# Local attention: the output projection in split halves for two batches at a time, values after the normed q and k, a second buffer for transposed q and k

## The chip, the cores and the metric

The kernel runs on one core of one Trainium2 chip, in one launch. The metric is the device time of that launch in microseconds (us). Engines are named PE (TensorE, matrix products; PEld is its loading of weights), DVE (VectorE), ACT (ScalarE), POOL (GpSimd) and SP (SyncE, which issues most DMAs).

## The reference, cut to what matters

The program is six blocks in a row on `x` of 64 batches x 128 tokens x 128 features, each with a layer norm in front and its input added behind. The third, the one that changes, is two layers of local attention with a gated feed-forward part:

```python
h = shift_token(x)                        # half of the features from the token before
q, k, v = jnp.split(h @ wqkv, 3, axis=-1) # 8 heads of 64
q = l2norm(q) * qs; k = l2norm(k) * ksc
q, k = rotary_xpos(q, k)
o = local_attention(q, k, v)              # a token sees itself and the 64 before it
x = x + o @ wo                            # 512 -> 128: the product that changes
h = layernorm(shift_token(x)) * lg + lb
a, g = jnp.split(h @ w1 + b1, 2, axis=-1)
x = x + (a * gelu(g)) @ w2 + b2
```

## The kernel before, in words

Each block is a class (B1 to B6), and each has a stage of the span to itself, but for its set-up, which runs within the stage ahead. All of `x` stays in SBUF. Stage 3 (class B3, line 1123) works on 16 chunks of 4 batches (`CB = 4`). For each chunk and each of the two layers there are four units, one a batch (`unit`, line 1182), and behind the fourth one the feed-forward part of the chunk (`ffn`, line 1246). That makes 32 chunk-layers and 128 units. `emit` (line 1296) starts one unit a step, layer 1 of a chunk two chunks behind its layer 0 (`LAG = 2`), and each `yield` in the text below moves what follows to a later step, so that some dozen units are under way at a time.

**Products.** A product in float32 is one call of `mm` and two records in the trace. Where speed matters, the kernel splits each float32 operand into a high and a low half of the type F32R, and `mm3` makes three products, high x high, high x low and low x high, that add up in PSUM. `wsplit` makes the halves of a weight: a copy and a subtraction on DVE. In stage 2 (B2) the output product is already made so, for two batches at a time: the tiles `ush`, `usl` and the weight `cBsh`, `cBsl`.

**A unit** (128 tokens, 8 heads) goes so: from the split input `yh`, `yl` come q and k (two PSUM tiles named B) and, right behind them, v (a PSUM tile named a), which ACT copies to `va` (8 buffers). ACT squares q and k (`fsq`); DVE sums the squares (`n2`) and makes the two rotary products `t1` and `t2`; POOL adds them, and scales them by the norm. D1 = 3 steps later PE transposes the result (`B<-k_eye,t`), and ACT copies it to `qkT`, which has one buffer. Then come the scores (`B<-qkT`) with the mask (`band`), the softmax (`mx`, `prob`, `dn` on DVE, ACT and POOL), its transposes (`probT` on ACT) and the product with `va`. ACT copies that to the tile `f_oT`, one for the four batches of a chunk.

**ffn**, behind the fourth unit, begins with the output projection: 4 float32 products of 512 columns over the whole chunk, which two DVE instructions of 64 x 512 add to the residual `ys`. Then it transposes, normalises, makes the two split products with `w1`, the gelu and the product with `w2`.

**Order.** Nothing of this runs in the order of the text. The calls are recorded (class `Recorder`) and, at the end of each stage, a planner (`order`) lays them out: each engine takes, of the instructions whose inputs and buffers are ready in its estimate, the one with the smallest position in the text plus an offset from a table (`PRIO`, by stage, engine and tile). PE's products are grouped up to 940 ns of estimate, and changes of the array's form and of ACT's function table carry penalties (`STICK`, `STICKX`, `STICKSET`). Each engine then works through its list strictly in order, so a late input holds what is listed behind it. SP issues DMAs in order too. All instructions are issued from one line of `flush` (L607), so the profile tells them apart by tiles.

PSUM has 8 banks: 5 for the tiles B and 3 for the tiles a. The input halves `yh`, `yl` have two buffers each, `t1` two, `t2` and `f_oT` one.

**Set-up of stage 3** runs in stage 2: `f_wo` is loaded as it is; `k_rot`, `k_band` and the two layers of `f_wqkv` pass one after the other through the single buffer `stage`; the two layers of `f_w1` through two buffers `stage1`.

Of the kernel before, what the change touches and what calls it, by code (L numbers as in the profile page):

```python
# [18 lines left out]
P = 128  # L19
NBATCH = 64  # L20
T = 128
# [28 lines left out]
H6, O6 = (2, 26)  # L50
LAG = 2
D1, D2, D3, D4 = (3, 1, 3, 1)
SIDES = ("left", "right")


def layout(inputs):
# [118 lines left out]
    for j, (s, g) in enumerate(((sc, 8.0), (1.0 / sc, 1.0))):  # L175
# [31 lines left out]
        "DVE:stage1<f_lg,stage1": -4000, "DVE:w1sh<stage1": -5400,  # L207
    },
    3: {
        "STICK": 1934, "STICKSET": 11024, "STICKX": -10655, "POOL:yl<yh,ys": 20400, "PE:B<wqsh,yh": 200,  # L210
        "PE:a<wqsh,yh": 1100, "ACT:va<a": 5600, "ACT:fsq<B": 37000, "DVE:n2<fsq": 500, "DVE:t1<B,rot": 9500,
        "DVE:t2<B,rot": 12900, "ACT:n2<n2": 68000, "DVE:ln6<xt": -19500, "DVE:lnmv<ln6": -5700,
        "ACT:lnr<eps5,lnmv": -32200, "ACT:lnr<lnr": -27600, "PE:a<htok,k_eye": -41300, "ACT:ys<a": 27300,
        "DVE:ys<a": -7000, "PE:B<k_eye,t1": 400, "ACT:qkT<B": -71200, "PE:B<qkT": 1100, "PE:B<band,eyeb": -45400,
        "DVE:mx<B": 3200, "DVE:dn<prob": 48100, "POOL:prob<dn,prob": 35200, "PE:B<k_eye,prob": -28500,
        "ACT:probT<B": 23000, "PE:a<probT,va": 8500, "ACT:f_oT<a": -68100, "DVE:ln6<a": -8400,
        "PE:a<ftok,k_eye": -33200, "ACT:fTh<a": -106100, "DVE:fTl<a,fTh": 8500, "PE:a<fTh,w1sh": 3000,
        "ACT:gl<a,f_b1": 15800, "ACT:gl<gl": 18200, "DVE:gl<a,f_b1,gl": -15300, "PE:a<f_w2,gl": 5700,
        "DVE:htok<a,f_b2,ys": 84900, "DVE:xt<a,xt": -1500, "PE:a<probT": 32400, "DVE:win0l<probT,win0h": 75300,
    },  # L220
    4: {
        "STICK": 22428, "STICKSET": 12816, "STICKX": -72497, "ACT:xTh<a": -25500, "DVE:xTl<a,xTh": 5000,
# [419 lines left out]
def build(tc, a, out, nb=NBATCH, blocks="123456"):  # L642
# [11 lines left out]
    def t(shape, tag, dt=F32, bufs=None):  # L654
        if isinstance(cur["wk"], Ahead):
            return nc.alloc(cur["wk"].pool, shape, dt, "ahead_" + tag, nm(tag), 1, 1)
        return nc.alloc(cur["wk"], shape, dt, tag, nm(tag), bufs, 2)
# [25 lines left out]
    def load(name, eng=None):  # L683
        ap = a[name]
        x = wt(ap.shape, name)
        (eng or nc.sync).dma_start(x, ap)
        return x
# [12 lines left out]
    def wsplit(parts, shape, name):  # L700

        hi, lo = wt(shape, name + "h", F32R), wt(shape, name + "l", F32R)
        for x, ix in parts:
            V.tensor_copy(hi[ix], x)
            V.tensor_tensor(lo[ix], x, hi[ix], ALU.subtract)
        return hi, lo
# [15 lines left out]
    def stage(ap):  # L722
        x = t(ap.shape, "stage", bufs=1)
        nc.sync.dma_start(x, ap)
        return x
# [397 lines left out]
    class B3(Block):  # L1123
# [2 lines left out]
        ahead = AH[1]  # L1126

        def load(s):
            s.wo, s.w2 = load("f_wo"), load("f_w2")
            s.lg, s.lb, s.b1, s.b2 = (load(n) for n in ("f_lg", "f_lb", "f_b1", "f_b2"))  # L1130

        def setup(s):
            s.rot = wt([P, 2, 2, 2, 64], "rot")
            krot, qsr = stage(a["k_rot"]), t([P, 2, 2, 64], "stage2", bufs=1)
            nc.sync.dma_start(qsr, a["f_qs"].to_broadcast([P, 2, 2, 64]))
            for l in range(2):
                for j in range(2):
                    V.tensor_tensor(s.rot[:, l, 0, j], krot[:, 0, j].rearrange("p a d -> p (a d)"),
                                    qsr[:, l, j], ALU.mult)
                    for u in range(2):  # L1140
                        V.tensor_tensor(s.rot[:, l, 1, j, 32 * u:32 * u + 32], krot[:, 1, j, u],
                                        qsr[:, l, j, 32 - 32 * u:64 - 32 * u], ALU.mult)
            s.band = cast(stage(a["k_band"]), "band", BF16)
            parts = []
            for l in range(2):
                w1 = t([P, 6, P], "stage1")
                nc.sync.dma_start(w1, a["f_w1"][:, l])
                p1 = ps("a")
                for g in range(6):
                    mm(p1[:, g:g + 1], w1[:, g], s.lb[:, l:l + 1])  # L1150
                V.tensor_tensor(s.b1[:, l], p1[:, 0:6], s.b1[:, l], ALU.add)
                V.tensor_scalar(w1, w1, s.lg[:, l:l + 1], None, ALU.mult)
                parts.append((w1, (slice(None), l)))
            s.w1 = wsplit(parts, [P, 2, 6, P], "w1s")
            s.wqkv = wsplit(((stage(a["f_wqkv"][:, l]), (slice(None), l)) for l in range(2)), [P, 2, 1536], "wqs")

        def halves(s, y):
# [24 lines left out]
        def unit(s, c, l, b):  # L1182
            d = s.d[c]
            hs = [x[:, b] for x in d["hs"]]
            qk, v = [ps("B"), ps("B")], ps("a")
            for j in range(2):
                mm3(qk[j], hs, [w[:, l, j * 512:(j + 1) * 512] for w in s.wqkv])
            mm3(v, hs, [w[:, l, 1024:1536] for w in s.wqkv])
            va = t([P, 8, 64], "va", bufs=8)
            nc.scalar.copy(va.rearrange("p h d -> p (h d)"), v)  # L1190
            sq = t([P, 2, 512], "fsq", bufs=1)
            for j in range(2):
                act(sq[:, j], qk[j], AF.Square)
            n2 = t([P, 16], "n2")
            V.tensor_reduce(n2, sq.rearrange("p j (h d) -> p (j h) d", h=8), AX.X, ALU.add)
            t1, t2 = t([P, 2, 8, 64], "t1"), t([P, 2, 8, 64], "t2", bufs=1)
            for j in range(2):
                V.tensor_tensor(t1[:, j], qk[j].rearrange("p (h d) -> p h d", h=8),
                                s.rot[:, l, 0, j].unsqueeze(1).to_broadcast([P, 8, 64]), ALU.mult)
                r4 = s.rot[:, l, 1, j].unsqueeze(1).to_broadcast([P, 8, 64]).rearrange("p h (u d) -> p h u d", u=2)  # L1200
                V.tensor_tensor(t2[:, j].rearrange("p h (u d) -> p h u d", u=2),
                                qk[j].rearrange("p (h u d) -> p h u d", h=8, u=2)[:, :, ::-1], r4, ALU.mult)
            G.tensor_tensor(t1, t1, t2, ALU.add)
            act(n2, n2, AF.Ln, bias=tiny)
            act(n2, n2, AF.Exp, scale=-0.5)
            G.tensor_scalar(n2, n2, 1e12, None, ALU.min)
            tv = t1.rearrange("p j h d -> p (j h) d")
            G.tensor_tensor(tv, tv, n2.unsqueeze(2).to_broadcast([P, 16, 64]), ALU.mult)
            for _ in range(D1):
                yield  # L1210
            qkT = t([P, 2, 4, T], "qkT", bufs=1)
            for j in range(2):
                tp = ps("B")
                for g in range(4):
                    tr(tp[:, g * T:(g + 1) * T], t1[:, j, 2 * g:2 * g + 2].rearrange("p h d -> p (h d)"), eye)
                nc.scalar.copy(qkT[:, j].rearrange("p g t -> p (g t)"), tp)
            for _ in range(D2):
                yield
            sc = [ps("B"), ps("B")]
            nc.join(True)  # L1220
            for g in range(4):
                for i in range(2):
                    r = slice(64 * i, 64 * i + 64)
                    mm(sc[i][:, g * T:(g + 1) * T], qkT[r, 0, g], qkT[r, 1, g], start=g == 0, stop=False)
            nc.join(False)
            for i in range(2):
                mm(sc[i], eyeb, s.band.unsqueeze(1).to_broadcast([P, 4, P]), start=False)
            p, dn = softmax8(sc, 1.0, T, (0, 1))
            normalise(p, dn, T)
            for _ in range(D3):  # L1230
                yield
            pt = transp8(p, T, "B")
            for _ in range(D4):
                yield
            u = ps("a")
            for g in range(4):
                for i in range(2):
                    mm(u[64 * i:64 * i + 64, g * T:(g + 1) * T], va[:, 2 * g + i], pt[:, 4 * i + g])
            if b == 0:
                d["oT"] = t([P, 4, W], "f_oT", bufs=1)  # L1240
            nc.scalar.copy(d["oT"][:, :, b * T:(b + 1) * T], u.rearrange("p (g t) -> p g t", g=4))
            if b == CB - 1:
                yield
                yield from s.ffn(c, l)

        def ffn(s, c, l):
            d = s.d[c]
            ys, yv = d["ys"], s.halves(d["ys"])
            w = ps("a")
            for g in range(4):  # L1250
                mm(w, s.wo[:, l, g], d["oT"][:, g], start=g == 0, stop=g == 3)
            w3 = w.rearrange("p (b t) -> p b t", b=CB)
            for i in range(2):
                V.tensor_tensor(yv[i], w3[64 * i:64 * i + 64], yv[i], ALU.add)
            yield
            p = ps("a")
            for b in range(CB):
                tr(p[:, b * T:(b + 1) * T], ys[:, b, 0:T], eye)
# [624 lines left out]
```

## Time and profile before

| what | value |
|---|---|
| median of 3 runs | 3488.49 us (3481.11 to 3489.39) |
| the profiled execution's own time | 3487.8 us |
| its span in the profile | 3486.0 us |
| granted PE clock, mean | 0.978 |
| stage 3: first to last product | about 1041 to 2351 us of the span |
| table loads on ACT between 1040 and 2340 us | 62, 79.5 us |

The page's first part gives each engine's busy time over the whole span. Those shares mix six stages with different limits; the tables by stretch give them for stage 3 alone. A row of the timeline has the start, the length, the engine, the line, the operation, the tiles written and read, the shape, and how many equal instructions were merged. A group by shape has busy time in all, the mean length in ns, and the engine's idle time just ahead of its instructions with what ended it. A row of the waits names the engine and tile that waited, what ended the wait, and the total, the number and the longest of such waits.

### The profile page before, as it was taken

The numbers are of one execution on the slowest core, as the hardware profiler recorded it, in microseconds if no ns is written. First come the engines' busy times: TensorE is split into PE (matmuls) and PEld (weight loads), VectorE is DVE, ScalarE is ACT, GpSimd is POOL, SyncE is SP. The second block draws the span as 40 slices with busy tenths as digits, with TensorE's granted clock in tenths as the row PEclk, the third lists the DMA queues.
The fourth block names the chain that finished last, engine by engine and source line by source line (L and its number), as shares of the span: only waits on it lengthen the run. The fifth ranks groups of instructions, "written<-read, shape, count | busy, mean of one in ns | idle before, by whom it ended". The sixth has DMA issues, their size and how long they took to land. (4 is left out here: it accounts for less than half of the span.)

```text
span 3486.0 us, 72432 instructions
## 1 busy us (share of the span) xinstructions
PE 3309.0 (95%) x26754; PEld 2504.7 (72%) x26754; DVE 3022.0 (87%) x6794; ACT 2587.3 (74%) x6272; POOL 1873.6 (54%) x1953
## 2 busy tenths in 40 slices
PE   5999999999998899999999999987999998999999
PEld 4877777777876677677777777755777776677776
DVE  7999788888878789888988888867999998999886
ACT  5888556666657788888888888855767775877785
POOL 2212023332328476676776766637899996544541
PEclk9999899999999999999999999997999998999999
DMA  5344210000000000000000000000000001000000
GB/s 133 88 91 98 68 46 20 10 15 10 14 6 1 1 1 1 1 1 1 1 1 1 1 1 1 1 20 7 1 1 1 1 1 31 10 16 19 16 11 16
DMA packets 43522, 67.13 MB, mean 19 GB/s; under 512 B 9520, under 2 KB 29330, under 8 KB 43171
## 3 DMA queue, kind: packets, MB, share of 16 engines
q1 hardware_dynamic: 42595, 61.98, 7.4%
q8 instruction: 213, 3.49, 0.4%
q14 instruction: 138, 1.13, 0.1%
q10 hardware_dynamic: 576, 0.53, 0.1%
HBM read 24.72 MB, written 4.19 MB: 8 GB/s over the span
## 5 line engine op out<-in xcount | busy, mean ns | idle before, releaser
L607 POOL TENSOR_TENSOR prob<-prob,dn 128x616 f32<-128x616 f32 (+1 forms) x256 | 398.9, 1558 | 471.6 <-DVE dn L607 181.1
L607 POOL TENSOR_TENSOR t<-t,t 128x1024 f32<-128x1024 f32 x128 | 304.7, 2381 | 265.4 <-DVE t L607 223.1
L607 DVE TENSOR_REDUCE dn<-prob 128x8 f32<-128x616 f32 (+1 forms) x384 | 356.6, 929 | 79.8 <-ACT prob L607 77.2
L607 DVE TENSOR_TENSOR t<-B,rot 128x512 f32<-128x512 f32 x512 | 331.6, 681 | 44.1 <-POOL t L607 19.5
L607 DVE TENSOR_REDUCE mx<-B 128x4 f32<-128x308 f32 (+1 forms) x512 | 281.7, 574 | 47.7 <-PE B L607 43.0
L607 ACT COPY probT<-B 77x512 f32<-77x512 f32 (+1 forms) x512 | 288.2, 617 | 36.1 <-PE B L607 31.3
L607 ACT ACTIVATE prob<-B,mx 128x128 f32<-128x128 f32 x1024 | 288.1, 392 | 24.7 <-DVE mx L607 24.2
L607 PEld LDWEIGHTS B<-k_eye,prob 128*77 128x77 f32 (+1 forms) x2048 | 234.6, 144 | 86.8 <-issue 44.9
L607 PE MATMUL B<-k_eye,prob 128*77 128x128 f32 (+1 forms) x2048 | 284.8, 276 | 4.6 <-ACT qkT L607 1.3
L607 POOL TENSOR_TENSOR probN<-prob,dn 128x512 f32<-128x512 f32 (+1 forms) x256 | 176.6, 714 | 141.6 <-PE s L607 104.8
L607 POOL TENSOR_TENSOR t<-t,n 128x1024 f32<-128x1024 f32 x128 | 243.6, 1903 | 4.8
L607 ACT ACTIVATE prob<-s,mx 128x77 f32<-128x77 f32 x768 | 190.8, 366 | 60.9 <-DVE mx L607 49.1
L607 ACT ACTIVATE prob<-prob 128x308 f32<-128x308 f32 x320 | 151.5, 483 | 88.7 <-DVE prob L607 87.5
L607 ACT ACTIVATE feat<-fp,fb 128x512 f32<-128x512 f32 x256 | 163.2, 708 | 33.8 <-PE fp L607 31.5
L607 ACT COPY qkT<-B 128x512 f32<-128x512 f32 x256 | 149.6, 590 | 48.9 <-PE B L607 47.2
L607 POOL TENSOR_TENSOR L<-gs,L 128x512 f32<-128x512 f32 x128 | 163.8, 1281 | 17.4 <-ACT gs L607 9.1
L607 PEld LDWEIGHTS B<-k_eye,t 128*128 128x128 f32 x1024 | 125.7, 142 | 63.7 <-issue 27.6
L607 DVE TENSOR_REDUCE n<-fsq 128x16 f32<-128x1024 f32 x128 | 154.8, 1209 | 16.2 <-ACT fsq L607 12.3
L607 DVE TENSOR_TENSOR am<-fp,k_tri 128x512 f32<-128x512 f32 x256 | 159.0, 675 | 6.7 <-PE fp L607 6.7
L607 POOL TENSOR_TENSOR qnl<-qn,qnh 128x512 fp32r<-128x512 f32 x32 | 44.9, 1407 | 221.8 <-ACT qnh L607 221.8
L607 PE MATMUL B<-ctxbd,qp 128*128 128x154 f32 x1024 | 164.0, 296 | 0.0
L607 DVE TENSOR_TENSOR_SCAN L<-x,k_eye 128x512 f32<-128x512 f32 x128 | 155.2, 1213 | 9.4 <-PE x L607 5.9
(389 smaller groups left out, 10691.0 us busy)
## 6 DMA issues: line engine op xcount, KB each, us to landing
qx<-qnh SPq DMA_DIRECT2D x128, 128.0 KB
qx<-qnl SPq DMA_DIRECT2D x128, 128.0 KB
ctxbd<-ctxbd SPq DMA_DIRECT2D x16, 308.0 KB
xt<-x SPq DMA_DIRECT2D x16, 256.0 KB
out<-xt SPq DMA_DIRECT2D x16, 256.0 KB
ctxT<-ctxT SPq DMA_DIRECT2D x16, 235.6 KB
stage<-f_wqkv SPq DMA_DIRECT2D x2, 768.0 KB
ctxk<-ctx SPq DMA_DIRECT2D x16, 77.0 KB
```

The costliest lines, as they stand in the source:

```text
L607: f(*a, **k)
```

## The change

- The output projection is made with split halves, for two batches at a time: ACT writes the high half `f_oTh`, DVE the low half `f_oTl`, and behind every second unit PE makes 4 x 3 products of 256 columns, which two DVE instructions of 64 x 256 add to the residual. It leaves `ffn` and stands at the end of `unit`.
- The weight `f_wo` is no longer loaded as it is, but through the buffer `stage` and split into `fwosh`, `fwosl`. `stage1` has one buffer in place of two.
- The product for v and its copy stand behind the norm and rotation of q and k, three steps later; `va` has 5 buffers in place of 8.
- `qkT` has two buffers in place of one.
- The table of offsets for stage 3 is another, so that the whole stage is laid out anew.

```diff
+VA, QKB, T2B = (5, 2, 1)
...
-            s.wo, s.w2 = load("f_wo"), load("f_w2")
+            s.w2 = load("f_w2")
...
-                w1 = t([P, 6, P], "stage1")
+                w1 = t([P, 6, P], "stage1", bufs=1)
...
+            s.wo = wsplit([(stage(a["f_wo"]), slice(None))], [P, 2, 4, P], "fwos")
...
-            qk, v = [ps("B"), ps("B")], ps("a")
+            qk = [ps("B"), ps("B")]
             for j in range(2):
                 mm3(qk[j], hs, [w[:, l, j * 512:(j + 1) * 512] for w in s.wqkv])
-            mm3(v, hs, [w[:, l, 1024:1536] for w in s.wqkv])
-            va = t([P, 8, 64], "va", bufs=8)
-            nc.scalar.copy(va.rearrange("p h d -> p (h d)"), v)
...
             for _ in range(D1):
                 yield
-            qkT = t([P, 2, 4, T], "qkT", bufs=1)
+            v = ps("a")
+            mm3(v, hs, [w[:, l, 1024:1536] for w in s.wqkv])
+            va = t([P, 8, 64], "va", bufs=VA)
+            nc.scalar.copy(va.rearrange("p h d -> p (h d)"), v)
+            qkT = t([P, 2, 4, T], "qkT", bufs=QKB)
...
-            if b == 0:
-                d["oT"] = t([P, 4, W], "f_oT", bufs=1)
-            nc.scalar.copy(d["oT"][:, :, b * T:(b + 1) * T], u.rearrange("p (g t) -> p g t", g=4))
+            if b % 2 == 0:
+                d["oT"] = [t([P, 4, 2 * T], n, F32R, 1) for n in ("f_oTh", "f_oTl")]
+            hi, lo = (x[:, :, b % 2 * T:b % 2 * T + T] for x in d["oT"])
+            u = u.rearrange("p (g t) -> p g t", g=4)
+            nc.scalar.copy(hi, u)
+            V.tensor_tensor(lo, u, hi, ALU.subtract)
+            if b % 2 == 0:
+                return
+            o = d["oT"]
+            yield
+            w, b2, yv = ps("a")[:, :2 * T], slice(b - 1, b + 1), s.halves(d["ys"])
+            for g in range(4):
+                mm3(w, [x[:, l, g] for x in s.wo], [x[:, g] for x in o], start=g == 0, stop=g == 3)
+            for i in range(2):
+                V.tensor_tensor(yv[i][:, b2], w[64 * i:64 * i + 64].rearrange("p (b t) -> p b t", b=2), yv[i][:, b2],
+                                ALU.add)
             if b == CB - 1:
                 yield
                 yield from s.ffn(c, l)
...
-            w = ps("a")
-            for g in range(4):
-                mm(w, s.wo[:, l, g], d["oT"][:, g], start=g == 0, stop=g == 3)
-            w3 = w.rearrange("p (b t) -> p b t", b=CB)
-            for i in range(2):
-                V.tensor_tensor(yv[i], w3[64 * i:64 * i + 64], yv[i], ALU.add)
-            yield
```

The table `PRIO[3]`, lines 209 to 220, is replaced as a whole; `STICK` goes from 1934 to 10959, `STICKSET` from 11024 to 49265, `STICKX` from -10655 to -74220.

More of the change, by code (lines that the diff above doesn't have):

```diff
@@ L209 @@
     3: {
[L210 to L219, printed above, removed]
+        "STICK": 10959, "STICKSET": 49265, "STICKX": -74220, "ACT:yh<ys": 8000, "PE:B<wqsh,yh": 16300,
+        "ACT:fsq<B": 218100, "DVE:n2<fsq": 27600, "DVE:t1<B,rot": 26700, "DVE:t2<B,rot": 23500,
+        "ACT:n2<n2,tiny": 3100, "DVE:ln6<xt": 49600, "ACT:lnr<eps5,lnmv": -112900, "ACT:lnr<lnr": 3700,
+        "DVE:htok<lnmv,lnr,xt": -12900, "PE:a<htok,k_eye": 7300, "ACT:ys<a": 26600, "DVE:ys<a": 4100,
+        "PE:a<wqsh,yh": 11500, "ACT:va<a": -23200, "PE:B<k_eye,t1": -400, "ACT:qkT<B": -198300, "PE:B<qkT": -4000,
+        "PE:B<band,eyeb": -900, "DVE:mx<B": -11400, "DVE:dn<prob": 81500, "DVE:dn<dn": 23600,
+        "PE:B<k_eye,prob": -50000, "ACT:probT<B": 10800, "PE:a<probT,va": -7300, "ACT:f_oTh<a": -128400,
+        "DVE:f_oTl<a,f_oTh": 8400, "PE:a<f_oTh,fwosh": -134500, "PE:a<f_oTl,fwosh": 1800, "DVE:ys<a,ys": -111900,
+        "PE:a<k_eye,ys": -17500, "DVE:ln6<a": -9100, "DVE:ftok<a,lnmv,lnr": -6600, "PE:a<ftok,k_eye": -7100,
+        "ACT:fTh<a": 6600, "DVE:fTl<a,fTh": 8700, "PE:a<fTh,w1sh": 7900, "ACT:gl<a,f_b1": -43500,
+        "DVE:gl<a,f_b1,gl": -6700, "PE:a<f_w2,gl": 4800, "DVE:bselb<k_bsel": -3700, "DVE:mF<a,m_gw": 61800,
+        "DVE:win0h<probT": 13100, "DVE:win1l<probT,win1h": 94700,
     },
@@ L1195, in unit @@
             V.tensor_reduce(n2, sq.rearrange("p j (h d) -> p (j h) d", h=8), AX.X, ALU.add)
-            t1, t2 = t([P, 2, 8, 64], "t1"), t([P, 2, 8, 64], "t2", bufs=1)
+            t1, t2 = t([P, 2, 8, 64], "t1"), t([P, 2, 8, 64], "t2", bufs=T2B)
             for j in range(2):
```

## The prediction

> **What bounds the kernel now.** I read the engines' busy line, then busy time by stretch of the span, then the starts of products in the timeline, then groups by shape, then the waits. First the busy line, and three stretches of stage 3 (local attention), the one that changes; its first product starts near 1041 us, its last ends near 2351 us:
>
> ```profile
> PE 3309.0 (95%) x26754; PEld 2504.7 (72%) x26754; DVE 3022.0 (87%) x6794; ACT 2587.3 (74%) x6272; POOL 1873.6 (54%) x1953
> ```
>
> ```profile
> 1150.00:2250.00 1100.00, 1075.07 (x7690) 782.48 (x7689) 961.62 (x1749) 937.86 (x2302) 734.48 (x480) 1.00 0.00 1
> ...
> 1041.00:1150.00 109.00, 97.94 (x720) 71.33 (x720) 90.06 (x146) 86.45 (x226) 78.27 (x50) 0.95 0.00 1
> 2250.00:2351.00 101.00, 86.00 (x538) 57.95 (x537) 73.47 (x145) 64.36 (x141) 38.11 (x25) 0.93 0.06 18
> ```
>
> Behind the length stand busy us of PE, PEld, DVE, ACT and POOL, then the granted clock. In the 1100 us of steady running PE idles 25 us at clock 1.00, DVE 138 us. Over the 1310 us of the stage DVE is busy 90.1 + 961.6 + 73.5 = 1125 us. So PE sets the pace, and DVE is close behind. PE's entries overlap, so a product is priced from its start to the next start:
>
> ```profile
> 1106.82 1.02 PE L607 MATMUL a<-f_oT,f_wo 128*128 128x512 f32 x2
> 1107.68 1.04 PE L607 MATMUL B<-k_eye,prob 128*128 128x128 f32 x8
> ```
>
> ```profile
> 605.24 0.37 PE L607 MATMUL a<-ush,cBsh 128*128 128x256 f32 x1
> 605.44 0.28 PE L607 MATMUL a<-usl,cBsh 128*128 128x256 f32 x1
> 605.56 0.28 PE L607 MATMUL a<-ush,cBsl 128*128 128x256 f32 x1
> ...
> 606.02 0.28 PE L607 MATMUL a<-ush,cBsh 128*128 128x256 f32 x1
> 606.14 0.40 PE L607 MATMUL a<-hTh,cAsh 128*128 128x512 f32 x1
> ```
>
> The first fence is one float32 product of today's output projection (two records, two passes): 1107.68 - 1106.82 = 0.86 us. The second is stage 2's own split product of two batches, the form that the change adds: the first of a run holds PE 0.20 us, each later one (606.14 - 605.44)/6 = 0.117 us. Now the DVE rows for the added work (stage 2 for usl and xt, stage 3 for ys; count, busy, mean ns), and who made PE wait in stage 3 (total us, times, longest):
>
> ```profile
> L607 DVE TENSOR_TENSOR ys<-a,ys 64x512 f32<-64x512 f32 x64 | 43.9, 687 | 10.6 <-PE a L607 10.0
> ```
>
> ```profile
> L607 DVE TENSOR_TENSOR usl<-a,ush 128x512 fp32r<-128x512 f32 x98 | 66.0, 683 | 8.6 <-ACT ush L607 8.4
> ...
> L607 DVE TENSOR_TENSOR xt<-a,xt 128x256 f32<-128x256 f32 x24 | 10.0, 415 | 1.5 <-PE a L607 1.5
> ```
>
> ```profile
> PEld B L607 <- ACT qkT L607: 37.4, 59, 2.3
> ...
> PE a L607 <- DVE ys L607: 10.3, 9, 2.6
> ...
> PE B L607 <- ACT qkT L607: 9.4, 15, 1.8
> ...
> PE a L607 <- DVE htok L607: 6.3, 10, 1.6
> ...
> PE a L607 <- DVE ftok L607: 3.5, 3, 2.5
> ```
>
> **Part by part.** All sums are against the profiled execution, 3487.8 us (span 3486.0); the median of the runs shown is 3488.49, so one figure serves for both within a microsecond.
>
> 1. Output projection on PE. Removed: 32 chunk-layers x 4 = 128 float32 products of 512 columns, 128 x 0.86 = 110.1 us. Added: 64 pairs of batches x 4 head pairs x 3 = 768 split products of 256 columns. In the built order of the changed program they stand in 126 runs (mostly of 7 and of 5), so 768 x 0.117 + 126 x (0.20 - 0.117) = 89.9 + 10.5 = 100.3 us. On the engine that sets the pace: **-9.8 us**. Bounds: the long runs alone, -20; every product at the 0.20 of a first one, 153.6 - 110.1 = +43.
>
> The loads of weights speak against this: 768 instead of 256. In stage 2's rows a load is 0.19 us long and the next starts 0.117 us later, so loads lie under the products. The Trainium skill ("TensorE: Matmul & The Clock Gate", Part 3) says that a weight load overlaps running products only where the row groups differ, and gives 107 ns for 128 columns (section LDWEIGHTS). By that rule 512 more loads would come to an estimated +55 us and this part to +45; the row speaks against the rule.
>
> 2. DVE. Added: 128 f_oTl subtractions (nearest row usl, 0.683 us) = 87.4 us, and 128 residual additions of 64x256 (nearest xt 128x256, 0.415 us) = 53.1 in place of 64 of 0.687 = 43.9. Together **+96.6 us of DVE**: 1125 + 96.6 = 1222 us in the stage. None of it is on PE; it fills idle DVE. Idle DVE in the stage falls from 185 us (1310 - 1125) to some 75. What PE pays is the lateness: its waits put down to DVE (10.3 + 6.3 + 3.5 = 20.1 us) I let grow with DVE's work, 96.6/1125 = 8.6%: **+1.7 us**. That is the least sure term. Its bounds are 0 and the first rival's price, since f_oTl stands in DVE's queue ahead of rotations, maxima and sums that PE's next products need.
>
> The Trainium skill ("Perfetto Trace Analysis", Identifying the Most-Contended Engine) would not call PE the bound: it rates VectorE by its occupancy (87% here) and TensorE by its weight loads (72%). By it nothing of part 1 shows and the whole +96.6 us of DVE does. The row of starts and PE's 25 idle us in 1100 say otherwise.
>
> 3. Two buffers of qkT. With one, ACT's copy for a batch must wait until PE has made the previous batch's scores. PE itself stood 9.4 us for ACT qkT; PEld another 37.4, mostly beneath running products. Not all of that is the buffer: part is ACT's queue. The order view shows how much the planner uses it: of 127 successive units, 108 had their first transposes placed before the previous unit's scores, and none its second; now 55 and 10. I take half of PE's own row: **-4.7 us**; bounds 0 and -46.8 (both rows).
>
> 4. Values behind q and k. The same 384 split products and 128 copies on ACT, three steps later. The split input yh, yl (two buffers) is held longer: its successor's copy and subtraction could be late, 0.65 + 1.19 us (their rows) for each of 32. Other batches' products cover them; without that cover +59 us. Fewer runs of split products elsewhere (355 to 302 in the built order) and more switches into half-array products (156 to 174 stretches) pull apart; I take 0.
>
> 5. ACT: f_oTh replaces f_oT, 0.594 us a copy against 0.585 for the ush copy of stage 2: 0. The same 103 table loads on ACT. POOL: no instruction more or less: 0.
>
> 6. Weights. f_wo's DMA (512 KB) moves behind k_band in the single stage buffer, f_wqkv behind it, and the second f_w1 load to the end of stage 2's SP queue, where it waits for the first half's split. Queued behind them are only loads of later context: f_wqkv's loads were issued at 505.5 and 522.4 us, over 500 us ahead of use. Splitting f_wo costs DVE 0.72 + 1.21 us (the 128x1024 rows of ew1s) between 500 and 600 us, where DVE idles 9%: 0; +1.9 without that cover.
>
> 7. The end of the stage. After the last context product PE now does 4 x 0.86 = 3.4 us in one block; then only the last pair's 12 x 0.117 + 0.17 = 1.6, plus f_oTl's 0.68 ahead of it: -1.2 us.
>
> Sum: -9.8 + 1.7 - 4.7 - 1.2 = -14.0; 3487.8 - 14.0 = **3474 us**. Its own range, 3465 to 3477, is part 1 or part 3 off by some us.
>
> **Rivals.**
>
> *DVE becomes the bound (slower).* With 1222 us of work, DVE must be busy 1222/1310 = 93.2% of the stage only to break even, and 1222/1296 = 94.3% for my forecast. The best 100 us of this stage:
>
> ```profile
> 1400.00:1500.00 100.00, 97.83 (x698) 70.83 (x697) 91.76 (x175) 84.01 (x208) 69.57 (x47) 1.00 0.01 1
> ```
>
> At 91.8% the stage takes 1222/0.918 = 1331 us, +21: 3509 us. For it: DVE works in order and stands for ACT and POOL. Against it, stage 4:
>
> ```profile
> 2500.00:2600.00 100.00, 94.16 (x723) 75.64 (x722) 94.48 (x207) 69.10 (x146) 91.41 (x147) 0.98 0.00 1
> 2600.00:2700.00 100.00, 95.72 (x752) 76.80 (x751) 96.48 (x223) 71.69 (x154) 94.98 (x151) 1.00 0.01 1
> ```
>
> There DVE holds 94 to 96% beside a busier POOL. It decides where DVE cannot pass 93.2%.
>
> *A wash (within 0.3%).* The qkT waits are ACT's queue and stay, and DVE's lateness takes some of part 1: -9.8 - 1.2 + 1.7 = -9.3 at best, 3478 to 3490, middle 3482.
>
> *More than counted (faster).* The second buffer removes both qkT rows, PEld's too: -9.8 - 46.8 - 1.2 + 1.7 = -56, 3432. Against it: PEld's waits lie mostly under PE's work, and PE idles only 25 us in the steady 1100.
>
> *It does not do what it says:* the buffer stays unused, which the 10 and 55 of 127 half suggest; its price is the wash.
>
> **How the numbers follow.** Within 0.3% means within 10.5 us, about what a measurement of this kernel can tell from no change. Forecast 0.40, wash 0.24, DVE bound 0.27, more than counted 0.09. The forecast's range ends at 3477, so it counts as faster: faster 0.49, same 0.24, slower 0.27. Both signs hold weight, so the range takes in the slower rival at 3509 and part of the larger gain: 3450 to 3512.
>
> **What would show it.** Part 1: a run of f_oTh, f_oTl products with starts 0.117 us apart and some 100 us in all between starts; wrong, if loads space them near 0.2. Part 2: f_oTl near 0.68 us and DVE in the steady stretch at 94% or more with PE's idle time not above 25 us in 1100; wrong, if PE's waits for DVE pass some 40 us. Part 3: PE's 9.4 us for qkT halves. Stages 1, 2, 4, 5 and 6 keep their lengths. The forecast is wrong altogether if the stage's length does not fall from 1310 to about 1296 us.

## The result, and the profile after

The changed kernel takes 3495.27 us in the median of 12 runs, beside 3487.62 for the kernel before (12 runs): 1.0026 of its time, 95% interval 1.0018 to 1.0034. It is 7.7 us slower where 14 us faster was forecast. The profiled execution took 3490.15 us (span 3487.7), which is near the fastest of its 12.

First the busy line, then the three stretches of stage 3 in the changed kernel (us, then busy time of PE, PEld, DVE, ACT and POOL, then the clock):

```profile
PE 3294.4 (94%) x27266; PEld 2549.2 (73%) x27266; DVE 3084.3 (88%) x6988; ACT 2579.9 (74%) x6272; POOL 1875.3 (54%) x1953
```

```profile
1041.00:1150.00 109.00, 96.97 (x755) 74.27 (x753) 93.35 (x175) 84.47 (x226) 76.83 (x50) 0.96 0.01 1
1150.00:2250.00 1100.00, 1062.53 (x8081) 820.76 (x8081) 1008.24 (x1880) 923.26 (x2276) 730.93 (x477) 1.00 0.01 1
2250.00:2351.00 101.00, 88.87 (x601) 64.97 (x600) 80.48 (x166) 68.68 (x159) 44.57 (x29) 0.94 0.06 18
```

In the steady 1100 us PE is now idle for 37 us where it was 25, and DVE is busy 91.7% where it was 87.4%. Over the three stretches DVE is busy for 1182 us where it was 1125. From the first product of q and k to the last with `f_w2` the stage takes 2359.2 - 1031.0 = 1328.2 us; it took 2351.9 - 1033.6 = 1318.3 (so it began some 7 us ahead of the 1041 us that I had written). The stage is 9.9 us longer. Behind it run the same instructions in the same order; 1128.5 us here against 1134.1 is the spread of single executions, since the same part took 1130 to 1141 us in the experiments that leave it alone.

The new projection in the timeline, a run of 7 and then one of 5 behind eight transposes:

```profile
1509.65 0.28 PE L610 MATMUL a<-f_oTh,fwosh 128*128 128x256 f32 x1
1509.77 0.28 PE L610 MATMUL a<-f_oTl,fwosh 128*128 128x256 f32 x1
...
1510.37 0.28 PE L610 MATMUL a<-f_oTh,fwosh 128*128 128x256 f32 x1
1510.48 1.04 PE L610 MATMUL B<-k_eye,prob 128*128 128x128 f32 x8
1511.28 0.37 PE L610 MATMUL a<-f_oTl,fwosh 128*128 128x256 f32 x1
1511.49 0.28 PE L610 MATMUL a<-f_oTh,fwosl 128*128 128x256 f32 x1
```

The starts are 0.12 us apart, and 0.21 behind the first of a run that follows transposes, as in stage 2. DVE's added work (count, busy, mean ns):

```profile
L610 DVE TENSOR_TENSOR f_oTl<-a,f_oTh 128x512 fp32r<-128x512 f32 x128 | 87.4, 683 | 14.0 <-ACT f_oTh L610 13.1
...
L610 DVE TENSOR_TENSOR ys<-a,ys 64x256 f32<-64x256 f32 x128 | 53.2, 416 | 9.1 <-PE a L610 8.2
```

And whom PE waited for between 1040 and 2340 us:

```profile
PE B L610 <- ACT qkT L610: 8.5, 18, 1.7
PE a L610 <- DVE ys L610: 7.3, 19, 1.2
PE a L610 <- ACT va L610: 5.2, 9, 1.0
PE B L610 <- ACT prob L610: 5.1, 8, 1.6
PE a L610 <- DVE gl L610: 4.9, 8, 0.9
PE B L610 <- ACT probT L610: 4.5, 10, 1.4
PE a L610 <- DVE f_oTl L610: 4.2, 6, 1.5
```

Two of these rows in the kernel before:

```profile
PE B L607 <- ACT prob L607: 1.9, 5, 0.8
...
PE a L607 <- ACT va L607: 0.5, 1, 0.5
```

The two lengths of DVE's added instructions came out as priced, 87.4 and 53.2 us. But in the timeline DVE's entries overlap as PE's do. In the kernel before, one of 0.68 us is followed 0.60 us later by the next:

```profile
1499.74 0.68 DVE L607 TENSOR_TENSOR t<-B,rot 128x512 f32<-128x512 f32 x1
1500.34 1.21 DVE L607 TENSOR_REDUCE n<-fsq 128x16 f32<-128x1024 f32 x1
```

So 97 us more in lengths is less in busy time: DVE's rose by 57 us (1125 to 1182) in the three stretches. Part of the difference is this overlap; the rest is not accounted for.

To see what became of PE's saving, I gave each run of equal products of stage 3 the time to the next run that is usual for its kind and its neighbours in the trace of before, the same table for both kernels. That sum is an estimate of PE's own work, and the rest of the stage is PE standing or slowed by waits. Work falls from 1217.7 to 1208.4 us (-9.3); the rest rises from 101 to 120 (+19). Other ways to sort the runs move these sizes by ten microseconds and more, but not their signs. The profile's own rows give a part of it: from the first product of the stage to the last, PE's idle time sums to 51.6 us before and 62.1 after. So PE has less work, and more than that was given back in waits.

### The profile page after: what moved, and what is told of

Read it like the earlier page. It is cut to its first block, busy times and chain, and to the rows that moved or that the text cites. A ratio compares the mean times of both kernels' runs of the same rounds, so it can differ in the third digit from the quotient of the medians.

```text
span 3487.7 us, 73683 instructions
## 1 busy us (share of the span) xinstructions
PE 3294.4 (94%) x27266; PEld 2549.2 (73%) x27266; DVE 3084.3 (88%) x6988; ACT 2579.9 (74%) x6272; POOL 1875.3 (54%) x1953
## 5 line engine op out<-in xcount | busy, mean ns | idle before, releaser
L610 ACT ACTIVATE prob<-B,mx 128x128 f32<-128x128 f32 x1024 | 299.4, 397 | 32.5 <-DVE mx L610 32.1
L610 ACT ACTIVATE fsq<-B 128x512 f32<-128x512 f32 x256 | 154.5, 619 | 19.7 <-DVE t L610 16.1
L610 PE MATMUL B<-qkT 64*128 64x128 f32 x2048 | 159.9, 287 | 5.7 <-ACT probT L610 1.7
L610 PE MATMUL B<-k_eye,t 128*128 128x128 f32 x1024 | 155.9, 278 | 9.4 <-ACT qkT L610 4.0
```

The source lines that it names most:

```text
L610: f(*a, **k)
```

## The experiments

**Theories.** A, load: DVE's added work (97 us by the lengths of its instructions) makes its other results late, and with them everything behind. B, direct wait: PE stands for the subtraction itself. C, layout: the new order of the stage is worse by itself. Q: late values and the second buffer of qkT gain something.

All ratios are to the kernel before on the same chip, with the 95% interval. The runs of different experiments were made on several chips.

### The same order, with the subtraction shortened or doubled

A planner that lays out the stage anew for each edit would hide a cost of 10 us. So in the kernels of this section the instructions are planned exactly as in the changed kernel, and only what is issued in their place differs; every engine's list keeps its order.

```diff
-                mm3(w, [x[:, l, g] for x in s.wo], [x[:, g] for x in o], start=g == 0, stop=g == 3)
+                mm(w, wh, o[0][:, g], g == 0, False)
+                shown(w, wh, o[1][:, g], o[0][:, g], False, False)   # planned with o[1], issued with o[0]
+                mm(w, wl, o[0][:, g], False, g == 3)
...
-            V.tensor_tensor(lo, u, hi, ALU.subtract)
+            nc.add("DVE", "tensor_tensor", lambda x, y, z, op: V.real.tensor_tensor(
+                x[:, :, :16], y[:, :, :16], z[:, :, :16], op), (lo, u, hi, ALU.subtract), {})
```

The first edit alone is same_order_no_low_read. With the second at 16, 64 or two full ones it is short, half and double.

> The changed kernel, every engine's list in the same order, but the second of each three projection products reads the high half in place of the low half (that part of the value is left out), so PE no longer waits for DVE's subtraction, which still runs in full. Theory A (load: the 97 us more on DVE make its other results late): 3495, as the changed kernel. Theory B (direct wait: PE stands for f_oTl itself, 7.3 + 4.2 us in the waits of the changed kernel): 3484. Theory C (layout: the new order of the stage is worse by itself): 3495.

Measured 3495.06, ratio 1.0016 (1.0007 to 1.0025). Against the changed kernel (1.0026) that is no change beyond the two intervals, and the 11 us of B are not there. B falls.

> As the run before, and DVE's subtraction covers 64 of its 512 columns (the rest of the low half is left out), about 0.13 us in place of 0.68: 70 us less DVE work in the same order of every list. Theory A: DVE is lighter and PE's idle time falls back to that of the kernel before, about 17 us less than the changed kernel: 3478. Theory B: as the run before, 3484. Theory C: 3492 to 3495, since the order is untouched.

Measured 3473.83, ratio 0.9958 (0.9946 to 0.9970): 21 us less than the run before. A's number; C cannot explain it, since no list moved. In the profiles the stage takes 1309.4 us here and 1330.5 in the run before. Who waited, in this kernel and then in the run before (between 1040 and 2340 us):

```profile
ACT prob L610 <- DVE mx L610: 22.3, 29, 1.7
ACT fsq L610 <- DVE t L610: 12.5, 21, 1.5
PE a L610 <- ACT va L610: 0.6, 1, 0.6
```

```profile
ACT prob L610 <- DVE mx L610: 31.9, 41, 2.2
ACT fsq L610 <- DVE t L610: 16.4, 31, 1.5
PE a L610 <- ACT va L610: 4.9, 8, 1.0
```

From the first product of the stage to the last, ACT's waits for DVE grow from 92.2 to 108.1 us and POOL's from 246.9 to 277.9. PE's own grow from 27.1 to 30.2 for DVE and from 18.0 to 26.6 for ACT. In PE's rows the lateness shows mostly under ACT's name.

A rival would be that the subtraction reads `u` in a PSUM bank, so that a shorter one gives the bank back sooner. PE's waits put down to `f_oTl` speak against it: 3.0 us here, 2.3 in the run before.

> As same_order_short_sub (the low half is not read), with the subtraction over 256 of 512 columns, about 0.41 us, in the same order of every list. In proportion (21 us for 70 us of DVE, measured): 0.27 us x 128 = 35 us less DVE work than the changed kernel, 3495 - 10 = 3485. If DVE decides only from a point near its full load: 3474 to 3478.

Measured 3480.16, ratio 0.9969 (0.9959 to 0.9979).

> As same_order_no_low_read, with the subtraction issued twice in a row, 87 us more DVE work in the same order of every list. In proportion: 3495 + 26 = 3521. If DVE is already the bound, all of it: 3495 + 87 = 3582.

Measured 3570.04, ratio 1.0230 (1.0216 to 1.0244). The subtractions took 27.9, 53.4, 87.5 and 176.1 us in all. The steady stretch of the short, half, full (no low read) and double kernels, one fence each:

```profile
1150.00:2250.00 1100.00, 1073.53 (x8184) 834.21 (x8184) 978.12 (x1909) 939.90 (x2321) 740.90 (x484) 1.00 0.00 1
```

```profile
1150.00:2250.00 1100.00, 1069.88 (x8158) 830.23 (x8157) 992.73 (x1896) 935.22 (x2305) 738.59 (x481) 1.00 0.01 1
```

```profile
1150.00:2250.00 1100.00, 1062.44 (x8065) 820.54 (x8063) 1007.00 (x1878) 924.10 (x2276) 730.05 (x477) 1.00 0.00 1
```

```profile
1150.00:2250.00 1100.00, 1022.02 (x7572) 774.90 (x7570) 1025.33 (x1897) 876.38 (x2151) 691.84 (x452) 1.00 0.00 1
```

The third busy number is DVE's: 88.9, 90.2, 91.5 and 93.2%. Each step of DVE work and what it cost the kernel, by the medians: 25.5 us cost 6.3 (a quarter), the next 34.1 cost 14.9 (0.44), the last 88.6 cost 75.0 (0.85). The runs come from two chips. By the ratios the three steps cost 4, 16 and 75 us, and by the length of the stage in the profiles (1309.4, 1314.5, 1330.5, 1403.7 us) 5, 16 and 73. So the first price is uncertain, some 0.15 to 0.25, and the other two hardly move. The price is not in proportion; it rises from less than a quarter to nearly all of the work as DVE goes from 89 to 93%. PE falls from 1074 to 1022 busy us meanwhile. The changed kernel sits in the middle of the bend. The bend belongs to this order of the stage: DVE is not full at 93%, since in stage 4 it was busy for 94 to 96% (the prediction's rows).

> The changed kernel in the same order of every list, with the subtraction and the second of each three projection products (low half of the attention output) planned but not issued: that part of the value is left out. Against same_order_short_sub (3474): DVE 28 us less, PE 256 products of 0.117 us, 30 us less. PE sets the pace: 3440. If the rest of DVE, ACT and POOL hold the stage as it is: 3465 or above.

Measured 3467.04, ratio 0.9938 (0.9924 to 0.9951). It beats both kernels, without the low half. But 30 us less PE work and 28 us less DVE work than the short kernel brought 6.8 us together (the two profiled executions lie 14 us apart). By the table of starts PE's work falls by the 30 us (1208.4 to 1178.4) and the rest of the stage rises from 101 to 116; PE's idle time in the profile rises from 50.6 to 67.9 us. With both of them relieved, something else in the fixed order holds the stage; which engine or wait it is, no run shows.

### One part alone, planned anew

> The kernel before, with the 128 subtractions of 128x512 added on DVE into a tile that nobody reads, laid out anew by the planner; the float32 projection stays. Theory A: the price of 87 us DVE work by itself, +17 to +20 us: 3505. Theory B: nobody waits for it, 3488 to 3491. Theory C: 3488 to 3491.

```diff
-            nc.scalar.copy(d["oT"][:, :, b * T:(b + 1) * T], u.rearrange("p (g t) -> p g t", g=4))
+            oT, u = d["oT"][:, :, b * T:(b + 1) * T], u.rearrange("p (g t) -> p g t", g=4)
+            nc.scalar.copy(oT, u)
+            V.tensor_tensor(t([P, 4, T], "f_oTl", bufs=1), u, oT, ALU.subtract)
```

Measured 3530.60, ratio 1.0121 (1.0106 to 1.0137): +41 us, A's direction and twice its number. DVE is busy for 90.4% of the steady stretch here, less than in the changed kernel, and the same subtraction costs twice as much. PE's waits for ACT qkT, which is no DVE instruction, go from 9.4 to 25.4 us.

> The kernel before, with the projection as 768 products of 256 columns in place of the 128 float32 ones, but the low half of the attention output left out (the high half is read twice), so no subtraction on DVE; values, qkT and offsets as before. All theories: PE's part alone, -9.8 us as the prediction priced it: 3478. If it is 3488, products of this form cost more in this stage than between starts in stage 2.

> The run 'before_plus_split_products' once more, with the offset that the table of before gives to the copy of the attention output (ACT:f_oT, -68100) kept for the copy under its new name; without it that copy stood later in ACT's list. The low half is left out as there. Theory A (DVE load alone explains the loss): PE's part is worth its -9.8, 3479. Theory C (layout): it stays near 3500, so that PE's part is lost to the order by itself.

```diff
-                d["oT"] = [t([P, 4, 2 * T], n, F32R, 1) for n in ("f_oTh", "f_oTl")]
+                d["oT"] = [t([P, 4, 2 * T], "f_oTh", F32R, 1)] * 2
...
-            V.tensor_tensor(lo, u, hi, ALU.subtract)
...
-    ... "ACT:f_oT<a": -68100,       # the second of the two kernels
+    ... "ACT:f_oTh<a": -68100,
```

Against the changed kernel's projection, put into the kernel before. The first gave 3499.98, ratio 1.0023 (1.0012 to 1.0035); its 12 runs lie between 3488 and 3504. The second gave 3476.27, ratio 0.9967 (0.9955 to 0.9979). The tile's new name had lost its entry in the table of offsets, and that alone hid the gain. With it the split products bring 11.6 us by themselves, close to the 9.8 of the prediction, where DVE has only the 9 us of the smaller additions more. Both kernels are planned anew, so the order may have a share in the 11.6.

> split_products_offset_kept (order, values and qkT as before, split products for two batches, no subtraction) with the product of the low half planned but not issued, the low half left out of the value: PE 30 us less than that run (3476): 3446 if PE sets the pace there, 3465 or above if not.

Measured 3471.71, ratio 0.9957 (0.9943 to 0.9971): 4.6 us less than the run that it is derived from, not 30. PE's idle time in the stage rises from 56.5 to 72.7 us. So already there, with DVE busy for 88.0% and no subtraction on it, PE's work alone does not set the pace.

> The kernel before with the whole new projection (split products for two batches, subtraction on DVE, weight through the stage buffer), but values, the one buffer of qkT and the table of offsets as before; the copy's offset kept under its new name, va with 7 buffers to make room. Theory A (PE's part -11.6, measured; DVE's load +21 as the same-order run has it): 3497. If DVE's load costs what the subtraction alone cost in the order of before (+41): 3517. If late values and the second buffer are what made the loss: 3478.

Measured 3540.26, ratio 1.0161 (1.0148 to 1.0175): 53 us, so the whole projection costs more in the order of before than the 41 us of the subtraction alone, although PE has less work. One buffer of va less is part of this run.

> The kernel before with values late (va 5 buffers) and two buffers of qkT, float32 projection and the table of before. Theory Q (these two gain by themselves): 3478 to 3484. Worth nothing by themselves: 3488. Theory C (they harm the order): above 3495.

Measured 3535.33, ratio 1.0144 (1.0130 to 1.0158). With the table of before, late values, the second buffer of qkT and 5 buffers of va together cost 48 us.

> The changed kernel with its projection put back: float32, four batches at a time, no subtraction; late values, two buffers of qkT and the new table of offsets stay. Theory Q (these parts gain by themselves): 3474 to 3482. If they are worth nothing: 3488. Theory C (the new order is worse by itself): 3495.

Measured 3502.84, ratio 1.0044 (1.0032 to 1.0057). Taking the projection back from the changed kernel does not gain the 10 us that the load would return (21 less 11.6). In this order, whose table was made for the split projection, the rest of the change is no gain without it.

> The changed kernel with one buffer of qkT, all else as it is. Theory Q: the second buffer saves about 4.7 us as predicted, so 3500. If the planner hardly uses it: 3495.

```diff
-VA, QKB, T2B = (5, 2, 1)
+VA, QKB, T2B = (5, 1, 1)
```

Measured 3515.89, ratio 1.0088 (1.0074 to 1.0102): the second buffer is worth 20.6 us in this kernel. PE's waits for ACT qkT rise from 8.5 to 20.0 us without it:

```profile
PE B L610 <- ACT qkT L610: 20.0, 30, 1.8
```

> The changed kernel with one penalty of the planner for stage 3 changed from 10959 to 11159: no more and no less work, only another order in some tenth of PE's list. It shows how much of a difference the order by itself can make: 3495 within 3 us if the order matters little, otherwise off by 10 or more.

Measured 3503.24, ratio 1.0053 (1.0040 to 1.0065): 8 us for an order that means nothing.

> The kernel before with one penalty of the planner for stage 3 changed from 1934 to 2134: the same work in a slightly other order. The shift on the changed kernel cost 8 us. If its table of offsets is fitted to its order as closely: 3492 to 3500; if the order of before is less delicate: 3487 within 3.

Measured 3489.65, ratio 1.0001 (0.9992 to 1.0011). The same shift on the kernel before costs nothing. Differences of this section below some 10 us are therefore not read as the price of a part.

### Other places for DVE's work

> The changed kernel, but the row sums of the softmax in stage 3 come from ACT's exponentials (each of them adds up its 128 columns beside its output) and not from 128 reductions of 128x1024 on DVE: 155 us less DVE work. Theory A: DVE falls below what it had before the change, PE's idle time falls to 98 us or less, 3474 or below, if ACT does the sums for nothing; with 0.1 us more for each of 1024 exponentials ACT, 86% busy, becomes the bound and it is 3500 or above. Theory C: 3495.

```diff
-                    act(pi[:, h], sv[:, h], AF.Exp, scale=scale, bias=m[:, i, h:h + 1])
+                    act(pi[:, h], sv[:, h], AF.Exp, scale=scale, bias=m[:, i, h:h + 1],
+                        **({"accum_out": d[:, 4 * i + h:4 * i + h + 1]} if len(biased) == 2 else {}))
...
-        V.tensor_reduce(d, p, AX.X, ALU.add)
+        if not summed:
+            V.tensor_reduce(d, p, AX.X, ALU.add)
```

Measured 3579.56, ratio 1.0267 (1.0253 to 1.0281). The edit also reached those exponentials of stage 5 that share the helper, so only stage 3 counts: 1359.0 us, 30.8 more than in the changed kernel. Two groups of ACT in the steady stretch tell why:

```profile
L610 ACT ACTIVATE prob<-B,mx 128x128 f32<-128x128 f32 x855 | 309.6, 392 | 19.6 <-DVE mx L610 19.2
L610 ACT ACTIVATION_READ_ACCUMULATOR prob<-B,mx 128x1 f32 x854 | 196.6, 231 | 0.0
```

Each sum costs ACT an instruction of 231 ns more, on an engine that was busy for 83.9% of this stretch in the changed kernel.

> The changed kernel with the low half's subtraction moved from DVE to POOL: ACT makes a second, float32 copy of the attention output in SBUF (128 copies of about 0.6 us, 76 us), POOL subtracts (128 x 1.2 us); va with 4 buffers to make room. 87 us less on DVE. Theory A: 21 us less, minus what ACT's load costs: 3474 to 3485, which would beat both kernels. If ACT, 86% busy, is as sensitive as DVE: 3495 or above.

```diff
-            V.tensor_tensor(lo, u, hi, ALU.subtract)
+            f = t([P, 4, T], "f_oT", bufs=1)
+            nc.scalar.copy(f, u)
+            G.tensor_tensor(lo, f, hi, ALU.subtract)
```

Measured 3522.06, ratio 1.0109 (1.0095 to 1.0123). That is 27 us more than the changed kernel: the work moved to ACT and POOL, the new order and one buffer of va less cost more than DVE's relief brings. The run does not part them.

> The changed kernel without the low half of the attention output (left out of the value): two products in place of three, no subtraction on DVE, planned anew with the same table. PE 256 products of 0.117 us less, 30 us, and DVE 87 us less. Theory A: 3495 - 21 - 30 = 3444. With the order's own spread of some 10 to 20 us: 3430 to 3465.

Measured 3483.43, ratio 0.9983 (0.9975 to 0.9992): 16 us above the same leaving-out in the fixed order, so the new plan took that much of it. It too beats both kernels, without the low half.

## Why the prediction was wrong, point by point

1. **PE's part, -9.8: the work was right, its worth is not shown in full.** The starts are 0.12 us apart, the first of a run 0.21; PE's work falls by 9.3 us by the table of starts, and the split products alone, planned anew, brought 11.6. But I counted each us that PE saves as a us of the stage. In a fixed order 30 us less of PE's work brought 4.6 us, so "PE sets the pace" held less than I wrote. The weight loads lie under the products here too (0.19 us long, one every 0.12 us), so the Trainium skill's rule on loads ("TensorE: Matmul & The Clock Gate", Part 3) again did not show.
2. **DVE's lateness, +1.7: this is the step that failed.** In the fixed order 60 of the 87 us of subtraction cost 21 us. The direction was right, and so was the warning that the term was the least sure. I took PE's waits put down to DVE and let them grow by 8.6%. The three rows that I scaled fell from 20.1 to 8.4 us, and all of PE's rows for DVE make 23.0 us before and 23.1 after, so the 40 us that I had named as the sign of being wrong did not come. What grew stands under other names: ACT va 0.5 to 5.2, ACT prob 1.9 to 5.1, ACT probT 0.2 to 4.5, while ACT f_oT fell from 6.5 to 1.2. The fixed order shows the same more cleanly: PE's waits for ACT grow by 8.6 us, for DVE by 3.1. These two make 12 of the 21 us; about as much again, 9 us, is PE busy for longer with the same products (1255.8 to 1264.9 us). A releaser is the last link; DVE's lateness reaches PE mostly through ACT, which waits for DVE's maxima and rotations first. A second size was off: the +96.6 us and the 1222 us are sums of lengths, and the busy time rose by 57 us to 1182, since entries overlap. So the shares of 93.2 and 94.3% that I drew from them were too high.
3. **Second buffer, -4.7: a wrong comparison.** PE's row for qkT is 8.5 us against 9.4; it did not halve. Yet without the buffer this kernel is 20.6 us slower. That fits a buffer that absorbs the lateness of a loaded DVE: with one buffer and the subtraction in the order of before, the row was 25.4 us. But no run has one buffer, this order and a light DVE, so it is not shown.
4. **Late values, 0: not settled.** In the order of before they cost 48 us together with the buffers; what they are worth in the new order was not measured. If -9.3 counts in full, it makes with +21 and a little for the last 28 us of DVE +12 to +17, and the kernel is +7.7. Then late values, buffer and new table together are worth some -4 to -9: a difference, not a run, and less than an order moves by itself.
5. **Set-up and the end of the stage, 0 and -1.2:** nothing in the runs contradicts them and nothing measures them; stage 3 begins 2.6 us earlier, within the spread of its start in the other runs (1027.8 to 1034.0).
6. **The rival "DVE becomes the bound"** had the direction and the engine, but its sum does not hold. It set 1222 us against a wall at 91.8%. DVE's busy time from the first product of the stage to the last is 1190 us, and 1190/0.918 = 1296 us would be no loss at all. Nor is 91.8% a wall: DVE goes to 93.2% here when pressed, and each further us then costs 0.85. That the stage took 1328 us where the rival had 1331 is luck. The +7.7 us of the kernel lie between the rival and the wash, within the 0.3% that I had called no change, at a chance of 0.24.

What stays open: why the subtraction costs 41 us in the order of before and 21 for most of it in the new one, although DVE's share is lower there (90.4 against 91.7%). One buffer of qkT and a table not made for it are both there, and one shifted offset alone moves the changed kernel by 8 us.

## What to carry to other kernels

Where a second engine is within a few per cent of the one that seems to set the pace, work added to it is not free until it is full. In this one order it cost up to a quarter of its time between 89 and 90% busy, 0.44 between 90 and 91.5 and 0.85 up to 93; in the other order about 0.47 with the engine at 90%. So expect a bend and not a wall, and don't scale up the waits under the engine's name, because its lateness shows as waits for whoever stands behind it. Price its instructions from start to start too: their lengths overlap. To measure one cost in a kernel whose order is planned, keep every list as it is and change only what is issued; anything planned anew can move by 10 us or more on its own, even by a renamed tile. And measure the gain in the same way: 30 us of work taken from the busiest engine brought 5.

## What the runs showed of the hardware that was not expected

- A sum taken along with an exponential on ACT is a second instruction of 231 ns behind each one of 392, where one DVE reduction of 128x1024 (1209 ns) makes the eight sums of a unit. Eight of the second instructions take 8 x 231 = 1848 ns.
- DVE's subtraction out of PSUM took 218 ns for 64 columns, 418 for 256 and 683 for 512: 1.04 ns a column, and some 150 ns whatever the size (683 - 512 x 1.04). Some 80 of them can lie under the next instruction: in the two DVE rows above, the entry of 0.68 us is followed after 0.60. Two 64x256 additions in place of one of 64x512 cost 2 x 416 against 687.
